# Two pairs of normed token tiles transposed by VectorE blocks and DMA through DRAM instead of TensorE, in a one-core transformer layer

## The chip, the cores and the metric

The kernel runs on one core of one Trainium2 chip. The metric is the device time of one execution, in microseconds (us). The notes below use the names that the profile uses: PE is TensorE (PEld its weight loads), DVE is VectorE, ACT is ScalarE, POOL is GpSimd, and SP is the engine that issues the DMAs of this kernel. "L118" is line 118 of the kernel before.

## The reference: what is computed

1024 tokens of width 512 (float32) pass through three sublayers, each behind a layer norm without weights:

```python
x = L0_attn_hidden_states                       # (4, 256, 512)
x = x + 0.5 * ffn(layernorm(x), A, B, Wr)       # 64 experts of rank 16, 16 of them taken per token
x = x + attn(layernorm(x), wq, wkv, wo)         # 32 heads of 128, causal
x = x + 0.5 * ffn(layernorm(x), A, B, Wr)

def ffn(x):     # per token
    scores = x @ Wr.T;  gates = softmax(top 16 scores);  G = gates placed at their experts
    h = x @ A (64 experts x 16);  out = (h * G) @ B;  return out * 2.0
```

The change lies between the first two sublayers: the normed tokens that the attention reads must be there with the width on the partitions, that is, transposed.

## The kernel before, in words

**Tiles.** The tokens are 8 tiles of 128, taken as 4 pairs. Everything is float32. The large products are made by Strassen-like schemes of seven products (M1 to M7) on sums of blocks, so each operand has to be cut into blocks and added up first.

**First feed-forward layer.** `ffn` (L274 on) runs the pairs through a software pipeline, `for u in range(n + 1)`. In one turn, PE does: the first product `ph_f` of pair u (L354, 7 products of two 128x512 matmuls), the transposes of the gated hidden values of pair u-1 (`pth_f`, L402, 4 groups of four), and its second product `po_f` (L422, 7 products of four 128x256 matmuls, in the order M1, M2, M6, M5, M7, M3, M4). In between lie the norm and router of pair u+1 (`ptx_f` L118, `pr_f` L338, the top-16 gates on DVE L285 to L308, their `exp` on ACT L301, gates L309) and, behind pair u-2, `norm_pair` (L528 on), which prepares the attention's operands. `po_f` M1 reads the block `a11` of `hgT`, M2 the block `a12`. Each block of `hgT` is copied from PSUM by ACT (L403), in the order a11, a21, a22, a12. The sums `hs_f` on DVE (L407 to L411) give M6, M5 and M3 their operands. ACT changes its function table twice in each turn, before the square root of the norms (L97) and before `exp` (L301).

**`norm_pair`.** Its first part makes the statistics (DVE L94, ACT L97 to L104) and writes the normed tokens of both tiles to slots 4 and 5 of `xop[5]` and `xop[6]` (ACT L111). Its second part has PE transpose each tile in four 128x128 matmuls against the identity (`ptx_a`, L118, into a PSUM tile of the pool `ps_t`, which has 2 buffers that `ptx_f` and three of the four `pth_f` groups use as well), and ACT copies the result into the operand blocks: pair 0 with two 128x256 copies per tile (L554, L555), pair 1 with four 128x128 copies per tile (L551, L552), after which DVE makes 8 block sums (`inner_sums`, L171 and the lines before it, called at L560). Pairs 2 and 3 do the same with DVE subtractions that read PSUM (L541 to L548).

**What sets the order.** In this layer a scheduler orders the instructions of each engine when the kernel is built; it may move them across the calls of the code. Each engine then takes its own in that order, and waits at the first that isn't ready. From the attention on, the order is written out by hand (`manual_schedule`) with due times. All DMAs of the kernel are issued by SP in one order. The last of the first layer is the store of the experts' sums (L253); behind it come the first attention weights `wqk` (L608), whose block sums POOL makes (L611).

**A transpose by blocks that is there already.** Late in the attention's `probs`, DVE transposes a 128x384 tile in 32x32 blocks (L1223), SP stores the four bands of 32 partitions to a DRAM tile (`moved`, L1226), and one load brings it back in full order (`pT`, L1232).

Of the kernel before, what the change touches and what calls it, by code (L numbers as in the profile page):

```python
# [9 lines left out]
F32 = mybir.dt.float32  # L10
# [4 lines left out]
P = 128  # L15
# [18 lines left out]
def macaron_kernel(  # L34
# [11 lines left out]
    nc = tc.nc  # L46
# [3 lines left out]
    scratch = ctx.enter_context(  # L50
        tc.tile_pool(name="scratch", bufs=1, space=bass.MemoryType.DRAM)
    )
# [11 lines left out]
    x = const.tile([P, NT, D], F32, tag="x", name="x")  # L64
# [42 lines left out]
    def normed(pool, ts, name, made=None):  # L107

        made = made or [pool.tile([P, D], F32, tag="xn", name=f"xn_{name}_{t}") for t in ts]
        for t, xn, (rstd, bias) in zip(ts, made, norm_stats(ts, f"{name}_{ts[0]}")):  # L110
            nc.scalar.activation(xn, x[:, t, :], AF.Identity, bias=bias, scale=rstd)  # L111
        return made

    def turned_x(xn, name):

        pt = ps_t.tile([P, DC, P], F32, tag="pt", name=f"ptx_{name}")
        for c in range(DC):
            nc.tensor.transpose(pt[:, c, :], xn[:, c * P : (c + 1) * P], ident)  # L118
        return pt

# [151 lines left out]
    def ffn(name, pairs, a_sums, b_sums, after, late, aside=None):  # L274


        with ExitStack() as scope:
# [34 lines left out]
            def prepare(pair):  # L312
# [4 lines left out]
                yield  # L317
                xt = work.tile([P, 2, DC, P], F32, tag="fxT", name=f"fxT_{n}")
                pt = [turned_x(tokens[i], f"{name}_{t}") for i, t in enumerate(pair)]
                for i in range(2):  # L320
                    nc.scalar.copy(xt[:, i], pt[i])
# [182 lines left out]
    xop = [xpool.tile([P, 7, S], F32, tag=f"x{o}", name=f"xop_{o}") for o in range(7)]  # L504


    early = [xop[o][:, 6] for o in (6, 5)]

    def inner_sums(o, eng, between=None):
        blocks = [xop[o][:, i] for i in range(4)]  # L510
        if o < 2:
            blocks[2] = early[o]
        left_sums(
            eng,
            [xop[o][:, i] for i in (4, 5, 6, 2)],
            *blocks,
            pinned=o > 1,
            between=between,
        )
# [8 lines left out]
    def norm_pair(work, pair):  # L528

        half, a = divmod(pair[0] // 2, 2)  # L530
        sl = slice(2 * a, 2 * a + 2)

        where = [xop[k][:, 4:6, :].rearrange("p a s -> p (a s)") for k in (5, 6)]
        tokens = normed(work, pair, "a", where)
        yield
        for i, xn in enumerate(tokens):
            cols = slice(i * P, (i + 1) * P)
            pt = turned_x(xn, f"a_{pair[i]}").rearrange("p (o c) k -> p o c k", o=2)
            a11, a12, s3, a22, s1, _, s2 = (xop[k][:, sl, cols] for k in range(7))
            if half:  # L540
                nc.scalar.copy(a22, pt[:, 1])  # L541
                if a:
                    nc.vector.tensor_tensor(s3[:, 0], early[0][:, cols], pt[:, 0, 0], ALU.subtract)
                    nc.vector.tensor_tensor(s3[:, 1], a11[:, 1], pt[:, 0, 1], ALU.subtract)
                else:
                    nc.vector.tensor_tensor(s3, a11, pt[:, 0], ALU.subtract)
                nc.vector.tensor_tensor(s2, pt[:, 1], s3, ALU.subtract)
                nc.vector.tensor_tensor(s1, a22, pt[:, 0], ALU.add)  # L548
            elif a:
                for o in range(2):  # L550
                    nc.scalar.copy(early[o][:, cols], pt[:, o, 0])  # L551
                    nc.scalar.copy(xop[o][:, 3, cols], pt[:, o, 1])  # L552
            else:
                nc.scalar.copy(a11, pt[:, 0])  # L554
                nc.scalar.copy(a12, pt[:, 1])  # L555
        if half and not a:
            nc.vector.tensor_tensor(xop[5][:, sl], xop[1][:, sl], xop[6][:, sl], ALU.subtract)
        elif a and not half:
            for o in range(2):
                inner_sums(o, nc.vector)  # L560
# [102 lines left out]
    with ExitStack() as scope:  # L663
        experts = load_experts(
            scope, "f1", "right", nc.vector, lambda i: load_x(range(4, NT) if i else (2, 3))
        )
        begin_v(0)
        load_all(("v", 0))
        first_layer = ffn(
            "f1",  # L670
            [(t, t + 1) for t in range(0, NT, 2)],
            *experts[:2],
            after=norm_pair,
            late=True,
            aside=lambda: sum_all(("v", 0), True),
        )
        take(first_layer, 3)
        experts[2]()
# [784 lines left out]
    for p in range(NG):  # L1463
# [34 lines left out]
        else:  # L1498
            steps = merged(p)
            share = sum(cost for _, cost in steps) / 8  # L1500
            parts, t = [[] for _ in range(8)], 0.0
# [130 lines left out]
```

## Time and profile before

| what | us |
|---|---|
| median of three runs (1125.55 to 1126.27) | 1126.14 |
| the profiled execution, its own time | 1124.15 |
| its span in the trace | 1122.3 |
| `ptx_a`: 4 transposes of pair 0, tile 0, start | 68.6 |
| `ptx_a` of pair 1, start | 92.5 |
| first `po_f` products of pairs 1 and 2, start | 72.9 and 100.6 |
| first product of the attention (`pv_a`), start | 127.7 |

The profile is one execution. A row of the groups gives line, engine, operation, tiles with their shapes, count, busy time and mean length. A row of the timeline or of the chain gives its start and length in us from the span's start. Matmuls are pipelined: a row of four transposes is 0.60 us long with its tail, and the next starts 0.44 us after it. The clock granted to TensorE is full speed in all 40 slices of the span. DMA is idle in the slices from 35 to 95 us. For the stretches around the change, the busy time of each engine is:

```profile
58.00:66.00 8.00, 8.00 (x30) 3.98 (x29) 2.78 (x8) 7.67 (x18) 1.06 (x1) 1.00 0.00 0
66.00:74.00 8.00, 8.00 (x49) 5.71 (x48) 4.97 (x28) 5.52 (x15) 2.42 (x3) 1.00 0.00 0
86.00:94.00 8.00, 7.87 (x29) 4.02 (x28) 2.40 (x8) 6.10 (x17) 1.06 (x1) 1.00 0.00 0
94.00:100.00 6.00, 6.00 (x24) 3.32 (x25) 6.00 (x14) 2.51 (x7) 1.06 (x1) 1.00 0.01 2
```

The columns of these rows: stretch and its length, then busy us and instructions of PE, PEld, DVE, ACT and POOL, the granted clock, the DMA engines' share, GB/s.

### The profile page before, as it was taken

The numbers are of one execution on the slowest core, as the hardware profiler recorded it, in microseconds if no ns is written. First come the engines' busy times: TensorE is split into PE (matmuls) and PEld (weight loads), VectorE is DVE, ScalarE is ACT, GpSimd is POOL, SyncE is SP. The second block draws the span as 40 slices with busy tenths as digits, with TensorE's granted clock in tenths as the row PEclk, the third lists the DMA queues.
The fourth block names the chain that finished last, engine by engine and source line by source line (L and its number), as shares of the span: only waits on it lengthen the run. The fifth ranks groups of instructions, "written<-read, shape, count | busy, mean of one in ns | idle before, by whom it ended". The sixth has DMA issues, their size and how long they took to land.

```text
span 1122.3 us, 21075 instructions
## 1 busy us (share of the span) xinstructions
PE 1110.7 (99%) x6834; PEld 977.4 (87%) x6834; DVE 807.3 (72%) x2234; ACT 441.9 (39%) x1328; POOL 626.5 (56%) x870
## 2 busy tenths in 40 slices
PE   9999999999999999999999999999999999999998
PEld 6666888899999999999999998999899999995767
DVE  5554677778778778778778778868778977865432
ACT  4453424444544544544544544544452000107310
POOL 4814487737887887887888788878532000002110
PEclk9999999999999999999999999999999999999999
DMA  9201020156756746746756756655799998750001
GB/s 332 86 1 38 29 67 16 31 145 197 203 138 195 210 136 193 207 136 192 203 152 174 210 144 183 190 166 161 205 311 321 335 348 264 243 180 1 19 19 38
DMA packets 198013, 180.06 MB, mean 160 GB/s; under 512 B 73488, under 2 KB 161296, under 8 KB 197648
## 3 DMA queue, kind: packets, MB, share of 16 engines
q1 hardware_dynamic: 197904, 178.72, 52.5%
q8 instruction: 55, 0.90, 0.3%
q14 instruction: 54, 0.44, 0.1%
HBM read 112.98 MB, written 65.67 MB: 159 GB/s over the span
## 4 chain that ended last, share of the span: by engine, by line
PE 90%; DMA 3%; DVE 2%; POOL 2%; SPq 1%; ACT 1%; issue 1%; POOLq 0%; DVEq 0%
PE po_M L1154 15%; PE po_f L422 9%; PE pqk_c L730 8%; PE ph_f L354 8%; PE pqk_b L730 8%; PE pqk_d L730 7%; PE pa L1255 5%; PE pv_c L829 4%; PE ps L1179 4%; PE pqk_a L730 3%; PE pv_b L829 3%; PE pa L1262 2%; PE ps L1178 2%; PE pv_d L829 2%; PE pv_e L829 2%; PE pv_a L829 2%
## 5 line engine op out<-in xcount | busy, mean ns | idle before, releaser
L384 POOL TENSOR_TENSOR hg_f<-hg_f,gate_f 128x512 f32<-128x512 f32 x32 | 33.5, 1059 | 259.5 <-ACT gate_f L309 151.1
L1154 PE MATMUL po_M<-or_M,ol_M 128*128 128x128 f32 x1456 | 164.7, 275 | 0.0
L1154 PEld LDWEIGHTS po_M<-or_M,ol_M 128*128 128x128 f32 x1456 | 163.7, 192 | 0.1
L611 POOL TENSOR_TENSOR wqk_M<-wqk_M 128x128 f32<-128x128 f32 x320 | 141.7, 458 | 12.1
L747 DVE TENSOR_TENSOR qk<-qk,pqk_d 128x512 f32<-128x512 f32 x210 | 116.6, 561 | 18.9 <-PE pqk_d L730 13.1
L611 POOL TENSOR_TENSOR wqk_M<-wqk_M,wqk_M 128x512 f32<-128x512 f32 (+1 forms) x64 | 107.2, 1683 | 38.7 <-DMA wqk_M<-in_wkv 23.0
L1199 ACT ACTIVATE s<-s,least 128x128 f32<-128x128 f32 (+1 forms) x256 | 114.3, 450 | 21.1 <-DVE least L1187 20.9
L1217 ACT ACTIVATE pn<-s,arden 128x128 f32<-128x128 f32 x220 | 93.7, 426 | 54.4 <-DVE arden L1208 50.7
L730 PE MATMUL pqk_c<-xop,wqk_M 128*128 128x256 f32 x448 | 111.3, 380 | 0.1
L730 PE MATMUL pqk_d<-xop,wqk_M 128*128 128x256 f32 x420 | 106.8, 381 | 1.1 <-DVE qk L747 1.1
L730 PE MATMUL pqk_b<-xop,wqk_M 128*128 128x256 f32 x420 | 104.0, 380 | 0.0
L747 DVE TENSOR_TENSOR qk<-qk,pqk_c 128x256 f32<-128x256 f32 (+1 forms) x112 | 59.7, 533 | 52.2 <-PE pqk_c L730 50.9
L1269 ACT COPY attn<-pa 128x256 f32<-128x256 f32 x128 | 47.4, 371 | 124.4 <-PE pa L1262 121.7
L1054 DVE TENSOR_TENSOR ol_M<-ol_M 128x512 f32<-128x512 f32 x104 | 75.1, 722 | 23.0 <-DMA ol_M<-left 22.6
L747 DVE TENSOR_TENSOR qk<-qk,pqk_b 128x512 f32<-128x512 f32 x105 | 71.7, 683 | 26.7 <-PE pqk_b L730 25.1
L730 PEld LDWEIGHTS pqk_c<-xop,wqk_M 128*128 128x128 f32 x448 | 78.7, 191 | 8.4 <-ACT qk L779 1.2
L1187 DVE CUSTOM_DVE_ANT_0 s<-ps,mask 128x128 f32<-128x128 f32 (+1 forms) x256 | 80.8, 353 | 3.8 <-PE ps L1179 2.6
L730 PEld LDWEIGHTS pqk_d<-xop,wqk_M 128*128 128x128 f32 x420 | 74.1, 191 | 9.9 <-DVE qk L747 2.9
L1255 PE MATMUL pa<-pT,vbuf 128*128 128x256 f32 x256 | 77.5, 384 | 3.4 <-DMA pT<-moved 2.5
L730 PEld LDWEIGHTS pqk_b<-xop,wqk_M 128*128 128x128 f32 x420 | 74.4, 191 | 7.2
L781 POOL TENSOR_TENSOR qk<-qk 128x256 f32<-128x256 f32 x64 | 46.6, 731 | 54.6 <-DVE qk L747 54.0
L1179 PE MATMUL ps<-qk 128*128 128x256 f32 x256 | 76.5, 380 | 0.0
(186 smaller groups left out, 2389.7 us busy)
## 6 DMA issues: line engine op xcount, KB each, us to landing
ol_M<-left SPq DMA_DIRECT2D x52, 512.0 KB, 5.8
moved<-s SPq DMA_DIRECT2D x440, 48.0 KB, 1.7
pT<-moved SPq DMA_DIRECT2D x110, 192.0 KB, 2.7
wv_M<-in_wkv SPq DMA_DIRECT2D x64, 128.0 KB, 2.6
wqk_M<-in_wq SPq DMA_DIRECT2D x64, 128.0 KB, 2.3
wqk_M<-in_wkv SPq DMA_DIRECT2D x64, 128.0 KB, 2.5
wo<-in_wo SPq DMA_DIRECT2D x16, 512.0 KB, 4.6
left<-attn SPq DMA_DIRECT2D x16, 512.0 KB, 3.3
```

The lines of the kernel that those rows point to most:

```text
L354: nc.tensor.matmul(ps, lhsT=left[m][:, c, :], rhs=a_right[m][:, c, :], start=first and c == 0, stop=c == 1, skip_group_check=True,)
L422: nc.tensor.matmul(ps[:, 0:256], lhsT=left[m][:, c, :], rhs=b_right[m][:, c, :], start=first and c == 0, stop=c == 3, skip_group_check=True,)
L611: return nc.gpsimd.tensor_tensor(to, a, b, ALU.subtract)
L730: nc.tensor.matmul(ps[:, i * S : (i + 1) * S], lhsT=right[m][n], rhs=xop[OUTER[m]][:, INNER[n]], start=first and i == 0, stop=True, skip_g ...
L747: nc.vector.tensor_tensor(to, of, ps, ALU.add)
L829: nc.tensor.matmul(ps[:, i * S + t * P : i * S + (t + 1) * P], lhsT=xop[OUTER[m]][:, INNER[n], t * P : (t + 1) * P], rhs=right[m][n], star ...
L1154: nc.tensor.matmul(banks[at // 2][:, cols : cols + P], lhsT=lhsT, rhs=rhs, start=k % 4 == 0 and g == 0 and at % 2 == 0 and t == 0, stop=Tr ...
L1179: nc.tensor.matmul(ps[:, P : 3 * P], lhsT=qT[:, P : 2 * P], rhs=kT, start=True, stop=True)
L1187: nc.vector.tensor_tensor_reduce(out=s[:, cols], in0=ps[:, cols], in1=mask_f[:, cols], scale=-SCALE, scalar=-TAKEN, op0=ALU.add, op1=ALU.m ...
L1199: nc.scalar.activation(s[:, cols], s[:, cols], AF.Exp, bias=least[:, i : i + 1], scale=-1.0, accum_out=den[:, i : i + 1],)
L1217: nc.scalar.mul(pn[:, :, i : 2 * i + 1, :].rearrange("p k t c -> p t k c"), s[:, cols].rearrange("p (t k c) -> p t k c", k=4, c=32), rden[ ...
L1255: nc.tensor.matmul(po[:, 0 : 2 * P], lhsT=v_of(p, j, 2 * b), rhs=of[:, 0:2], start=True, stop=False,)
```

## The change

For pairs 0 and 1 (`half` is 0), the first part of `norm_pair` now also moves each tile: DVE transposes the 128x512 tile in 32x32 blocks from `xop[5]` or `xop[6]` to slots 4 and 5 of `xop[2]` or `xop[3]`; SP stores its four bands of 32 partitions to a DRAM tile `moved_x` (64 KB each), and one load of 256 KB brings it back to where the normed tokens were. The PE transposes `ptx_a` of these two pairs are gone, and with them four uses of the PSUM pool `ps_t`. ACT makes the same number of copies with the same sizes, from SBUF instead of PSUM. Pairs 2 and 3 are left as they were.

```diff
+    def move_x(xn, blocks, name):
+        moved = scratch.tile([P, 4, P], F32, tag="moved_x", name=f"moved_x_{name}", bufs=4)
+        nc.vector.transpose(
+            blocks.rearrange("p (q c r) -> p q c r", q=4, r=32),
+            xn.rearrange("p (c q r) -> p q c r", q=4, r=32),
+        )
+        for t in range(4):
+            nc.sync.dma_start(
+                moved[:, t].rearrange("(q r) x -> r q x", r=32),
+                blocks[32 * t : 32 * t + 32].rearrange("r (q x) -> r q x", q=4),
+            )
+        nc.sync.dma_start(xn, moved.rearrange("p t x -> p (t x)"))
...
         tokens = normed(work, pair, "a", where)
+        if not half:
+            for i, xn in enumerate(tokens):
+                move_x(xn, xop[2 + i][:, 4:6, :].rearrange("p a s -> p (a s)"), f"a_{pair[i]}")
         yield
         for i, xn in enumerate(tokens):
             cols = slice(i * P, (i + 1) * P)
-            pt = turned_x(xn, f"a_{pair[i]}").rearrange("p (o c) k -> p o c k", o=2)
+            if half:
+                pt = turned_x(xn, f"a_{pair[i]}").rearrange("p (o c) k -> p o c k", o=2)
+            else:
+                pt = xn.rearrange("p (t o c x) -> p o c t x", t=4, o=2, x=32)
...
             elif a:
                 for o in range(2):
-                    nc.scalar.copy(early[o][:, cols], pt[:, o, 0])
-                    nc.scalar.copy(xop[o][:, 3, cols], pt[:, o, 1])
+                    for to, k in ((early[o], 0), (xop[o][:, 3], 1)):
+                        nc.scalar.copy(to[:, cols].rearrange("p (t x) -> p t x", t=4), pt[:, o, k])
             else:
-                nc.scalar.copy(a11, pt[:, 0])
-                nc.scalar.copy(a12, pt[:, 1])
+                for to, k in ((a11, 0), (a12, 1)):
+                    nc.scalar.copy(to.rearrange("p c (t x) -> p c t x", t=4), pt[:, k])
```

The scheduler builds a new order from this, on PE, DVE, ACT and SP, between about 59 us and the first product of the attention; ahead of it and behind it, and on POOL throughout, the orders are the same. In the new order:

- **DVE** has the two block transposes of a pair right behind the reciprocal of its norm (L101). For pair 0 this is ahead of the norm statistics of the first layer's last pair (tiles 6 and 7); for pair 1, ahead of the `hs_f` sums of pair 2. The 8 block sums of `inner_sums` come behind the first two `po_f` additions of pair 2 instead of ahead of its `hs_f` sums.
- **ACT**, around pair 0: the copies `hg_f`, `hg_f`, `hgT_f` (a11), then the norm of tiles 6 and 7, two `fxT_f` copies, `hgT_f` (a21), the first operand copy of pair 0, the table load, two `exp`, the second operand copy, `hgT_f` (a22), two gates, the third and fourth operand copies, `hgT_f` (a12), `hg_f`. Before, a21, `hg_f`, a22 and a12 were next to each other behind the gates. Around pair 1: the four `hgT_f` copies, four operand copies, one `hg_f`, four operand copies.
- **PE**, around pair 0: `pth_f` (one group), four `ph_f` matmuls, eight `ptx_f`, one `ph_f`, `pr_f`, `pth_f`, one `ph_f`, two `pth_f` groups, then `po_f`.
- **SP**: the 20 DMAs of `move_x` lie between L253 and the first `wqk` load. Within a pair the order is four stores of the first tile, three of the second, the load of the first, the last store of the second, the load of the second.

## The prediction

> **What bounds the kernel now.** I read the page's busy times first, then the chain that ended last, then that chain in order of time around the change, then ACT, DVE and SP in the timeline of the same stretch.
>
> ```profile
> PE 1110.7 (99%) x6834; PEld 977.4 (87%) x6834; DVE 807.3 (72%) x2234; ACT 441.9 (39%) x1328; POOL 626.5 (56%) x870
> PE 90%; DMA 3%; DVE 2%; POOL 2%; SPq 1%; ACT 1%; issue 1%; POOLq 0%; DVEq 0%
> ```
>
> PE is busy nearly all the time and carries 90% of the chain, so what is taken from PE is gained, unless a wait takes its place. The chain from 41 us on shows one such wait, then the stretch of pair 0 (`ptx_a` at 68.60 and 69.91) and that of pair 1 (92.47):
>
> ```profile
> 42.36 1.28 ACT L301
> 43.65 0.55 ACT pr_f L301 x2
> 44.21 1.00 ACT hgT_f L403 x2
> ...
> 62.75 0.44 PE pth_f L402 x4
> 63.19 0.91 PE ph_f L354 x2
> 64.10 0.61 PE ptx_f L118 x4
> ...
> 68.60 0.44 PE ptx_a L118 x4
> 69.05 0.86 PE ph_f L354 x2
> 69.91 0.44 PE ptx_a L118 x4
> ...
> 73.37 0.48 PE pth_f L402 x4
> 73.85 11.76 PE po_f L422 x54
> 85.61 6.87 PE ph_f L354 x16
> 92.47 0.87 PE ptx_a L118 x8
> ...
> 100.58 12.09 PE po_f L422 x56
> ```
>
> From 62.75 on PE doesn't stop. At 42 to 45 us it does: there the table load and the two `exp` stand ahead of two `hgT_f` copies on ACT, and PE waited 0.84 us for them. SP is free between these two rows of its timeline, which is where the new DMAs go:
>
> ```profile
> 30.29 0.33 SPq L253 DMA_DIRECT2D kept_b<-bt_f  x1
> 98.89 0.37 SPq L608 DMA_DIRECT2D wqk_M<-in_wq  x1
> ```
>
> **What is removed: 16 transposes on PE.** In the chain, 4 take 0.44 us, 8 take 0.87; two pairs make 0.44 + 0.44 + 0.87 = 1.75 us on the path. Here a rule has to be weighed. The Trainium skill, TensorE: Matmul & The Clock Gate, Part 4 (PE-mode transpose), gives about 390 ns for a 128x128 transpose alone and about 275 ns within a kernel. The rows agree with the 275 (`ptx_a` has a mean of 275 ns), but that is the length of one with its tail, and the next starts 110 ns later. By the page's numbers 16 would be worth 4.4 to 6.2 us, by the rows 1.75. I take 1.75. The new order also puts fewer changes of operation on PE. In the stretch of pair 0, rows that are longer than their kind (0.91 for 0.86 twice, 0.61 for 0.44, 0.48 for 0.44) hold 0.31 us of small waits; in that of pair 1 it is 0.13 of "issue" and 0.19 in a `pth_f` row, again 0.3. These may go or return: 0 to 0.62 us.
>
> **What is added on DVE: four block transposes of 128x512.** The nearest row is the one of 128x384 in the attention, which reads PSUM:
>
> ```profile
> L1223 DVE STREAM_TRANSPOSE s<-pn x110: 574/577/580, 220.7 to 804.7; 128x384 f32<-128x384 f32 x110
> ```
>
> Bounds for 512 columns: 0.58 us (no dependence on size) and 0.77 (in proportion); I take 0.71. They wait for ACT's normed tokens, so in pair 0 the first runs from 61.5, the second from 62.2 to 62.9. Queued behind them on DVE are the statistics of tiles 6 and 7, which before ran from 60.1 to 61.8. They now take 62.9 to 64.5; the square root, reciprocal and biases on ACT and DVE end at 65.5, and the normed tiles on ACT at 66.3 and 67.0 (0.8 us each, starts 0.7 apart). PE reaches `ptx_f` in its new order at 62.75 + 0.44 + 4 x 0.86 = 66.63 and 67.07. So this cover holds, with 0.3 and 0.07 us to spare; at 0.77 us each the second would be 0.05 late. In pair 1 they run from 91.25 to 92.65 with the `hs_f` sums behind them, which wait for ACT until 94.5 anyway: nothing.
>
> **What is added on SP and DMA.** In the attention four such stores are issued in 1.76 us, land 1.7 us after issue (median; 1.6 to 4.8), and the load lands after 2.7 (2.3 to 5.4). Those move 48 and 192 KB; 64 and 256 KB in an idle stretch I put at 1.7 and 2.9. Pair 0: seven stores from 62.2 to 65.3, the fourth landed at 65.2, first load 65.3 to 68.2; last store at 65.7, landed 67.4, second load to 70.3. ACT comes to the first copy at 71.0 and to the third at 74.4, so the DMAs are covered by 2.8 and 4.1 us. Pair 1: transposes ended at 91.95 and 92.65, loads landed at 98.1 and 100.5. ACT then makes the eight copies by 101.3. DVE needs them for the block sums at 103.3, behind the addition of M2; the sums (8 x 0.335 us) end at 106.0, and the addition of M6 queued behind them at 106.4, just when PE wants that bank for M7 (106.4). Nothing, but with no cover left: a load 2 us later would stop PE. Behind the DMAs on SP stand the `wqk` loads; SP is free for them at 97.8, before 98.89, so they don't move.
>
> Against this way stands the Trainium skill, VectorE: DVE Perf Modes, Rules for kernel authors: a 128x128 transpose belongs on TensorE where PSUM will do as a target, and VectorE is for 32x32. The rows say why it needn't hold here: DVE has free time (2.8 of 8 us busy from 58 to 66) and PE none.
>
> **What moves: the copies on ACT, and this becomes a wait.** PE in the new order, from 62.75 with the lengths of the rows: `pth_f` 0.44, four `ph_f` 3.44, `ptx_f` 0.88, `ph_f` 0.86, `pr_f` 1.68, `pth_f` 0.44 (ends 70.49), `ph_f` 0.86, `pth_f` 0.88 (72.23), `po_f` M1 1.74: 73.97. M2 then reads a12. ACT: a21 from 70.5, next start 0.5 later; first operand copy 71.0 (0.38); table load 1.28; two `exp` 0.5; second operand copy 0.27; a22 0.5; two gates 0.5; two operand copies 0.54; a12 0.59, done at 75.6. That is a wait of 1.65 us for M2, the same kind as the 0.84 at 42 to 45 us. Before, M2 began at 73.85 + 6 x 0.218 = 75.16. So M2 starts 75.6 instead of 75.16, about 0.45 later, although PE has 0.88 less to do. M6 wants an `hs_f` sum at 77.3 that is done at 75.7: covered. If the table load took the 2.7 us of the Trainium skill, ScalarE: Activation LUTs, Table sets, M2 would start at 77.0; all rows of this trace say 1.28, which I take.
>
> For pair 1 there is no table load in between, and the four `hgT_f` copies come first: a12 is done at 95.7 and needed at 101. PE from 92.47: three `pth_f` groups, `ph_f`, `pth_f`, three `ph_f`, half of M1, two `ph_f`, rest of M1, together 8.65 us, so M2 at 101.1 instead of 100.58 + 1.73 = 102.3, a gain of 1.2 if the small waits vanish, 0.9 if they return.
>
> **Sum.** -1.75 for the transposes, -0.62 to 0 for the small waits, +1.65 for M2: -0.7 to -0.1, I take -0.4. Behind 130 us the orders are the same, and POOL's chain that follows (163 to 183 us) starts from products of PE, so the difference is carried to the end. The profiled execution (1124.15, its span and 1.85 us around it) would go to 1123.75; the median lies 1.99 above, hence 1125.7.
>
> **Rivals.**
> - **The wait doesn't form** (0.12). ACT would have to have a12 by 74. For it: before, ACT was idle 2.45 us at 66 to 69. Against: a12's copy stands behind nine others and a table load. Then -1.75 to -2.4: 1124.0.
> - **A longer wait at M2** (0.20). The 0.07 us of cover of `ptx_f` fails, copies from SBUF with runs of 32 are slower than the 0.37 us from PSUM, small waits return. Four copies of 0.2 more and 0.5 on PE's way to `pth_f` give +1.3: 1127.0.
> - **The round trip comes late, slower than before** (0.10). Place: the first and third operand copy of pair 0 on ACT, with `exp` and the `hgT_f` copies behind them. It decides from the moment a load lands after 71.0 or 74.4. At the longest landings seen in the attention (4.8 and 5.4 us) the first load lands at 73.7 and the second at 78.9, M2 waits 4.5 us more: 1130.2. Against: those landings are under 150 to 220 GB/s, here DMA is idle.
> - **The change doesn't do what it says**: the built order has no `ptx_a` left for these pairs; no chance kept.
>
> **How the numbers follow.** Likeliest, 0.58: 1125.7. About 0.2% (2.25 us) is what a measurement of this kernel can tell from no change. Faster by that needs 1123.9, which only the first rival in full can give: 0.05. Slower needs 1128.4: the late round trip and a tail of the longer wait, 0.13. Within it: 0.82. The range leaves out the late round trip and the last of the full gain: 1124.0 to 1127.9.
>
> **What would show it.** Right: an idle time of PE in front of a `po_f` row at about 74 us, ended by ACT `hgT_f`, of 1.2 to 2 us; ACT's copies of pair 0 not ended by a DMA; block transposes of about 0.7 us; no wait at 106 us. Wrong: ACT's operand copies waiting for `moved_x`, PE waiting at `ptx_f`, or the difference arising behind 130 us.

## The result, and the profile after

| | before | after |
|---|---|---|
| median of five runs each, us | 1125.66 (1124.39 to 1126.27) | 1131.48 (1130.12 to 1132.01) |
| the profiled execution, its own time, us | 1124.15 | 1130.17 |
| its span, us | 1122.3 | 1128.4 |

The ratio is 1.0057, with a 95% interval of 1.0046 to 1.0067: slower by 5 to 7.5 us, where 1125.7 was forecast and 1127.9 was the upper end of the range.

The page of the changed kernel has PE busy for 0.8 us less than before, and less of the chain on PE; DVE, ACT and DMA each have a point more of it.

```profile
PE 1109.9 (98%) x6818; PEld 975.9 (86%) x6818; DVE 813.0 (72%) x2238; ACT 443.0 (39%) x1328; POOL 626.3 (56%) x870
PE 89%; DMA 4%; DVE 3%; ACT 2%; POOL 2%; SPq 1%; issue 1%; POOLq 0%; DVEq 0%; ACTq 0%
```

Its chain in order of time (start, length, what) answers to the rows from 62.75 on that the prediction shows. Lines are shifted: L354 is now L369, L402 L417, L422 L437; L418 is the `hgT_f` copy, L576 an operand copy of pair 0, L186 a block sum, L449 the addition of a `po_f` product to `x`.

```profile
67.62 0.66 PE ptx_f L118 x4
...
71.35 0.59 ACT hgT_f L418
71.94 0.30 ACT xop L576
...
72.26 1.28 ACT L316
...
75.41 0.60 ACT xop L576 x2
76.00 0.49 ACT hgT_f L418
...
76.54 10.63 PE po_f L437 x48
87.16 6.87 PE ph_f L369 x16
...
104.46 0.42 DVE x L449
104.88 4.79 DVE xop L186 x8
109.67 0.34 DVE x L449
...
110.05 1.99 PE po_f L437 x8
```

The chain leaves PE twice. From 71 to 76.5 us it runs over ACT, which is the wait for M2 that was predicted. From 104.5 to 110 it runs over DVE: eight block sums take 4.79 us and hold up the addition that frees the bank of M7. The timeline of PE has both waits with their lengths, in the brackets:

```profile
76.54 1.78 PE L437 MATMUL po_f<-b_f,hgT_f 128*128 128x256 f32 x7 [1.76 <-ACT hgT_f L418]
...
110.05 1.99 PE L437 MATMUL po_f<-bt_f,hgT_f 128*128 128x256 f32 x8 [2.07 <-DVE x L449]
```

Where the 6.1 us of the span come from is read off four marks: the first `pth_f` of the second pair's hidden values, the first `ph_f` of the next turn, the first product of the attention (`pv_a`), and the end.

| stretch | before | after | difference |
|---|---|---|---|
| start to `pth_f` (62.59, 63.13), nothing changed here | 62.59 | 63.13 | +0.5 |
| turn of pair 0, to `ph_f` (85.44, 87.00) | 22.85 | 23.87 | +1.0 |
| turn of pair 1, to `pv_a` (127.53, 130.30) | 42.09 | 43.30 | +1.2 |
| attention to the end | 994.8 | 998.1 | +3.3 |

The first is from one execution to the next: in the 14 traces of this study in which nothing is changed ahead of it, that mark lies from 62.1 to 63.4. So the change itself lost 2.2 us where it was made. In this pair of traces the larger part, 3.3 us, lies behind 130 us, where the orders are the same as before; two traces can't size that part well, as the table of experiments shows.

### The profile page after: what moved, and what is told of

The parts are those of the page before. It is cut to its first block, busy times and chain, and to the rows that moved or that the text cites. A ratio compares the mean times of both kernels' runs of the same rounds, so it can differ in the third digit from the quotient of the medians.

```text
span 1128.4 us, 21070 instructions
## 1 busy us (share of the span) xinstructions
PE 1109.9 (98%) x6818; PEld 975.9 (86%) x6818; DVE 813.0 (72%) x2238; ACT 443.0 (39%) x1328; POOL 626.3 (56%) x870
## 4 chain that ended last, share of the span: by engine, by line
PE 89%; DMA 4%; DVE 3%; ACT 2%; POOL 2%; SPq 1%; issue 1%; POOLq 0%; DVEq 0%; ACTq 0%
PE po_M L1175 15%; PE pqk_b L751 8%; PE pqk_c L751 8%; PE ph_f L369 8%; PE po_f L437 8%; PE pqk_d L751 7%; PE pa L1276 5%; PE pv_c L850 4%; PE ps L1200 4%; PE pqk_a L751 4%; PE pv_b L850 3%; PE pa L1283 2%; PE ps L1199 2%; PE pv_a L850 2%; PE pv_d L850 2%; PE pv_e L850 2%
## 5 line engine op out<-in xcount | busy, mean ns | idle before, releaser
L632 POOL TENSOR_TENSOR wqk_M<-wqk_M 128x128 f32<-128x128 f32 x320 | 142.3, 459 | 12.1
L632 POOL TENSOR_TENSOR wqk_M<-wqk_M,wqk_M 128x512 f32<-128x512 f32 (+1 forms) x64 | 107.4, 1688 | 42.1 <-DMA wqk_M<-in_wkv 25.2
L1200 PE MATMUL ps<-qk 128*128 128x256 f32 x256 | 76.5, 380 | 0.0
```

What stands on the lines that cost most here:

```text
L632: return nc.gpsimd.tensor_tensor(to, a, b, ALU.subtract)
L1200: nc.tensor.matmul(ps[:, P : 3 * P], lhsT=qT[:, P : 2 * P], rhs=kT, start=True, stop=True)
```

## The experiments

In the table, "turns" is the time from `pth_f` to `pv_a` (64.94 before), and "attention" that from the first to the last copy of an attention product (693.4 before). Both are from one trace each; the ratio is against the kernel before, run beside it; it is estimated from all executions and need not be that of the two medians.

| kernel | us, before beside it | ratio, 95% | turns | attention |
|---|---|---|---|---|
| changed kernel | 1131.48, 1125.66 | 1.0057 (1.0046 to 1.0067) | 67.2 | 696.4 |
| pair0_only | 1127.99, 1124.92 | 1.0024 (1.0014 to 1.0034) | 65.9 | 695.4 |
| pair1_only | 1128.53, 1124.92 | 1.0034 (1.0021 to 1.0047) | 67.9 | 696.4 |
| same_addresses | 1131.26, 1124.92 | 1.0052 (1.0036 to 1.0067) | 68.9 | 695.3 |
| gap_1MiB | 1124.94, 1124.92 | 1.0001 (0.9993 to 1.0009) | 64.9 | 693.7 |
| pool_waits | 1126.54, 1124.50 | 1.0020 (1.0014 to 1.0027) | 65.1 | 694.7 |
| copies_and_sums_late | 1127.22, 1124.50 | 1.0027 (1.0016 to 1.0038) | 65.7 | 694.9 |
| dmas_only | 1125.61, 1124.50 | 1.0011 (1.0002 to 1.0019) | 64.9 | 695.0 |
| delay_only | 1126.83, 1124.50 | 1.0018 (1.0011 to 1.0024) | 67.9 | 693.3 |
| order_by_hand | 1127.46, 1125.47 | 1.0020 (1.0012 to 1.0029) | 63.3 | 697.0 |
| dmas_twice | 1125.29, 1125.47 | 1.0002 (0.9992 to 1.0012) | 64.9 | 696.8 |
| dmas_small | 1124.47, 1125.47 | 1.0000 (0.9990 to 1.0010) | 64.9 | 694.8 |
| dmas_early | 1125.82, 1125.47 | 1.0002 (0.9992 to 1.0012) | 64.9 | 694.5 |
| order_by_hand_padded | 1126.44, 1125.04 | 1.0011 (1.0003 to 1.0019) | 63.3 | 697.0 |
| dve_six_more | 1125.93, 1125.04 | 1.0010 (1.0001 to 1.0018) | 64.9 | 695.5 |
| pe_fourteen_less | 1130.40, 1125.04 | 1.0044 (1.0030 to 1.0057) | 64.9 | 695.7 |
| pe_64_more | 1131.24, 1125.04 | 1.0052 (1.0038 to 1.0066) | 64.9 | 695.5 |

The last two kernels start later by 3.4 and 5.9 us at the first mark, which the two last columns don't contain. The turns of pair1_only and same_addresses contain 1.7 us of a lower clock, told below. The last column has to be read with care: the ten traces without the change (the kernel before included) lie from 693.3 to 696.8, the eight with it from 694.7 to 697.0, so that no single trace separates them. The ratios do: less what the turns, the start and the lower clock explain, they leave 1.7 to 3.9 us behind `pv_a` with the change, and -0.9 to 1.6 without it.

### One pair at a time

```diff
-        if not half:
+        if not half and not a:
             for i, xn in enumerate(tokens):
...
-            if half:
+            if not (not half and not a):
                 pt = turned_x(xn, f"a_{pair[i]}").rearrange("p (o c) k -> p o c k", o=2)
```

This is pair0_only; pair1_only has `a` for `not a`. The other pair is transposed on PE again.

> Only pair 0 is moved by VectorE and DMA; pair 1 is transposed by TensorE as before. The traces show two local losses: M2 of the second product of pair 1 starts about 1.0 us later against the start of that turn (its operand copy stands behind the table load and the operand copies on ScalarE), and TensorE waits 2.07 us for a VectorE addition behind the block sums of pair 1. Theory 1 (the losses are local and each belongs to its pair): this kernel keeps the first alone: the wait of 1.76 us ended by ScalarE hgT_f is there, the wait of 2.07 us is not, and at the first product of the attention it is about 1.0 us later than before. Theory 2 (the two pairs interact, for instance the first delay makes the second collision): neither this nor the kernel with pair 1 alone shows the wait of 2.07 us. For the whole time: 1.0 us over before if all is local, 3 to 4 us if what the attention adds (about 3 us in the first trace) comes with any such DMA or with the moved DRAM tiles.

> Only pair 1 is moved by VectorE and DMA. Theory 1 (local losses): TensorE gains about 1.2 us up to the second product of pair 2 and then waits about 2 us there for the VectorE addition behind the block sums, which take about 0.8 us each in their middle, since GpSimd's weight sums run at that time, instead of 0.35; at the first product of the attention it is 0.9 us later than before, and ScalarE shows no new wait at the first product's turn of pair 0. Theory 2 (interaction): no wait there, so 1.2 us earlier than before. For the whole time: 0.9 us over before if all is local, 3 to 4 us if the attention adds its part here too.

Measured: 1.0024 and 1.0034; the two losses, 2.7 and 3.8 us, add up to the 6.4 of both (0.0057 of 1125). pair0_only has the wait at M2 (1.76 us) and none at M7, with 1.0 us more in the turns; pair1_only has the wait of 2.07 us at M7 and none at M2. So each wait belongs to its pair. In both the attention of the trace is 2 to 3 us longer.

### The DRAM tile: where the attention's tiles lie

The new tile `moved_x` shifts the attention's DRAM tiles by 1 MiB. One kernel has the new order with the old addresses (`moved_x` lies in rows of the output that are written later), the other the old order with the shift.

```diff
-        moved = scratch.tile([P, 4, P], F32, tag="moved_x", name=f"moved_x_{name}", bufs=4)
+        at = int(name.split("_")[1]) * P
+        moved = out[at : at + P].rearrange("p (t x) -> p t x", t=4)
```

```diff
         take(first_layer, 3)
         experts[2]()
+        gap = scratch.tile([P, 4, 4, P], F32, tag="gap", name="gap")
+        nc.sync.dma_start(gap[:, 0, 0, 0:64], wr_sb[:, 0, :])
```

> The changed kernel, with its orders of instructions on all engines, but the blocks pass through the rows of the output tensor (written with the result at the end) instead of tiles of their own in DRAM. So every later DRAM tile of the attention has the address that it has in the kernel before; in the changed kernel these are 1 MiB higher. Theory A (what the attention adds, about 3 us, comes from the addresses): about 2.2 us over before, with the two local waits, and an attention as long as before. Theory B (it comes with the later phase or with the 20 DMAs, not with the addresses): about 5.8 us over before, like the changed kernel.

> The kernel before, with its orders of instructions, plus a DRAM tile of 1 MiB that nothing reads (one store of 32 KB goes to it at a time when no DMA runs), so that the later DRAM tiles of the attention have the addresses of the changed kernel. Theory A (addresses): about 3 us over before, all of it in the attention, with TensorE waiting longer for the loads of pT. Theory B: like before, within 0.5 us.

Measured: 1.0052 with the old addresses, like the changed kernel; 1.0001 with the shift alone (at most 0.0009, or 1.0 us). The addresses are not the cause.

The trace of same_addresses showed something else. Its timeline of PE around M7, with the wait in brackets:

```profile
109.98 2.88 PE L438 MATMUL po_f<-bt_f,hgT_f 128*128 128x256 f32 x8 [2.07 <-DVE x L450]
112.65 2.73 PE L438 MATMUL po_f<-b_f,hs_f 128*128 128x256 f32 x8
115.22 1.89 PE L438 MATMUL po_f<-bt_f,hgT_f 128*128 128x256 f32 x8
```

Eight such matmuls take 1.89 us with their tail, 1.99 right behind a wait. The first two rows take 2.88 and 2.73: 1.7 us are lost once more, since the clock that was granted fell to half. The busy times of the engines around it, with the columns as for the kernel before (the granted clock is the third number from the end):

```profile
107.50:110.90 3.40, 1.33 (x7) 0.91 (x6) 2.76 (x6) 0.00 (x0) 3.08 (x7) 1.00 0.00 0
110.95:114.35 3.40, 3.40 (x9) 2.66 (x8) 0.42 (x1) 0.00 (x0) 3.32 (x8) 0.50 0.00 0
114.40:117.80 3.40, 3.40 (x21) 3.04 (x20) 1.07 (x3) 0.32 (x1) 3.40 (x6) 1.00 0.02 5
```

The trace of pair1_only has the same from 109.35 to 112.76, 3.68 us for the row behind the wait. The clock does not fall every time: 2 of the 5 executions of the changed kernel, 4 of 6 of same_addresses and 1 of 6 of pair1_only have a mean clock of 0.998, none of the 21 of pool_waits below. In same_addresses those four take 1130.7 to 1133.3 us, the other two 1128.2 and 1128.3. The profiled execution of the changed kernel is one without it.

The traces show what decides. In them the clock changes only in steps of 3.413 us: its stretches, the last of a trace aside, are whole numbers of these, such as 102.40, 105.81, 1116.16 and 3.413 us (30, 31, 327 and 1). Counted in such steps from the first rise of the clock (at 5.12 us in same_addresses, 6.95 in pair1_only and 6.67 in the changed kernel), the pause of 2.07 us lies within one step in the first two, and the next step ran at half the clock. In the changed kernel it is divided between two steps, 1.09 and 0.98 us, and the clock stayed. The pause of 1.76 us at M2 lies within one step in three traces (pair0_only, same_addresses, pool_waits), and the clock stayed there too. If the place of the pause is left to chance, it lies within one step in (3.41 - 2.07) / 3.41 = 39% of the executions (an estimate); seen were 7 of 17, if the pause is behind all of these. A mean of 0.998 also stands in one execution each of pair0_only, of order_by_hand_padded and of the kernel before (of 158), which have no such pause; where their clock fell is not known.

### Who slows the block sums

The theory after the first runs: GpSimd. Its sums of the first attention weights (`wqk_M`, L632) run at the same time as DVE's block sums, which they did not before. The rival: the sums are slow because they come right after the copies and the DMAs of pair 1. In one kernel GpSimd waits for the last block sum (a small copy reads it, and `True` keeps the first weight sum behind that copy); in the other the sums and the copies of pair 0 come later in the code, with GpSimd left alone.

```diff
     load_all(("qk", 0))
+    seen = const.tile([P, 1], F32, tag="seen", name="seen")
+    tc.keep_in_program_order(nc.gpsimd.tensor_copy(seen, xop[1][:, 2, 0:1]))
-    sum_all(("qk", 0))
+    sum_all(("qk", 0), True)
```

```diff
                     take(steps, 8)
+                    take(behind, 1)
...
         yield
+        if not half and not a:
+            yield
         for i, xn in enumerate(tokens):
...
         elif a and not half:
+            yield
+            yield
             for o in range(2):
```

> The changed kernel with one small copy more on GpSimd (128x1), which reads the last of the block sums of pair 1 and stands ahead of GpSimd's first weight sums of the attention, so that GpSimd is idle while VectorE makes the block sums. All other orders are the same. Theory A (the middle block sums take 0.8 us instead of 0.35 because GpSimd adds from the same memory at that time): all eight take 0.34 to 0.42 us each, the addition of M6 comes 2 us earlier, and TensorE's wait of 2.07 us ahead of M7 shrinks to under 0.3 us; whole time about 2 us less than the changed kernel, 3 to 4 us over before. Theory B (they are slow for another reason, such as what the DMA brought or which operands they read): they stay at 0.8 us and the wait stays.

> The changed kernel with two of its steps placed later: the second to fourth operand copies of pair 0 stand behind all hgT_f copies on ScalarE, and the addition of M6 stands between the block sums of pair 1 on VectorE instead of behind them. Theory A (local waits of the two turns): the wait ahead of M2 falls from 1.8 us to about 1.2 (the table load and one operand copy still stand ahead), that of 2.07 us goes; TensorE is at the attention's first product within 0.5 us of before, and the whole time is 2.5 to 3 us less than the changed kernel. If the attention's part (2 to 3 us more than before in all kernels with the moves so far) is a thing of its own, 2 to 3 us over before stay. Rival (the attention's part follows from the lateness at its start): nothing over before stays.

First the kernel before: the block sums on DVE, while GpSimd has nothing between 91 and 98 us, and then the first weight sums on GpSimd:

```profile
93.98 1.09 DVE L171 TENSOR_TENSOR xop<-xop,xop 128x256 f32<-128x256 f32 x3 [4.06 <-ACT xop L551]
94.99 1.42 DVE L171 TENSOR_TENSOR xop<-xop 128x256 f32<-128x256 f32 x4
96.33 0.41 DVE L171 TENSOR_TENSOR xop<-xop,xop 128x256 f32<-128x256 f32 x1
...
103.51 1.28 POOL L611 TENSOR_TENSOR wqk_M<-wqk_M,wqk_M 128x512 f32<-128x512 f32 x1
104.86 3.84 POOL L611 TENSOR_TENSOR wqk_M<-wqk_M 128x128 f32<-128x128 f32 x8
```

In the changed kernel, DVE:

```profile
104.79 1.09 DVE L186 TENSOR_TENSOR xop<-xop,xop 128x256 f32<-128x256 f32 x3
105.80 3.27 DVE L186 TENSOR_TENSOR xop<-xop 128x256 f32<-128x256 f32 x4
109.00 0.67 DVE L186 TENSOR_TENSOR xop<-xop,xop 128x256 f32<-128x256 f32 x1
109.59 0.74 DVE L449 TENSOR_TENSOR x<-x,po_f 128x256 f32<-128x256 f32 x2
```

and GpSimd:

```profile
105.54 1.47 POOL L632 TENSOR_TENSOR wqk_M<-wqk_M,wqk_M 128x512 f32<-128x512 f32 x1 [1.41 <-DMA wqk_M<-in_wkv]
107.09 4.37 POOL L632 TENSOR_TENSOR wqk_M<-wqk_M 128x128 f32<-128x128 f32 x8
```

The row of four sums hides two kinds. The first two of them, and the GpSimd sum between, looked at alone:

```profile
105.80 1.49 DVE L186 TENSOR_TENSOR xop<-xop 128x256 f32<-128x256 f32 x1
107.21 0.67 DVE L186 TENSOR_TENSOR xop<-xop 128x256 f32<-128x256 f32 x1
107.09 0.52 POOL L632 TENSOR_TENSOR wqk_M<-wqk_M 128x128 f32<-128x128 f32 x1
```

Both inputs of a block sum lie in `xop`. The first three sums take 1.09 us as before. From 105.54 on, when GpSimd begins, four take 3.27 instead of 1.42. GpSimd is slowed too: 1.47 and 4.37 us for what takes 1.27 and 3.83 alone. But DVE's two additions at 109.59, one of whose inputs is in PSUM, take 0.74 us together, no longer than usual (0.42 for one, the next 0.33 behind it), although GpSimd is still busy. In pool_waits, DVE and then GpSimd:

```profile
104.28 1.09 DVE L186 TENSOR_TENSOR xop<-xop,xop 128x256 f32<-128x256 f32 x3
105.28 1.43 DVE L186 TENSOR_TENSOR xop<-xop 128x256 f32<-128x256 f32 x4
```

```profile
107.11 0.18 POOL L1296 COPY seen<-xop 128x1 f32<-128x1 f32 x1 [3.50 <-DVE xop L186]
107.31 1.27 POOL L632 TENSOR_TENSOR wqk_M<-wqk_M,wqk_M 128x512 f32<-128x512 f32 x1
108.66 3.83 POOL L632 TENSOR_TENSOR wqk_M<-wqk_M 128x128 f32<-128x128 f32 x8
```

With GpSimd held back, all eight sums are at their old speed at the same place, behind the same copies and DMAs; PE reaches M7 at 107.43 without a wait, and the kernel is at 1.0020. In copies_and_sums_late GpSimd begins 0.37 us behind the first sum, so the first three already take 2.16 us, and 0.66 us of wait stay at M7. The theory holds, the rival falls. The Trainium skill, SBUF — State Buffer, section SBUF: two separate sides, has the rule for this: DVE and GpSimd share a pair of SBUF ports, and a DVE operation with two SBUF inputs and a GpSimd operation that reads SBUF shut each other out for the whole instruction. The rows agree in kind: the sum of 105.80 ends 0.28 us behind GpSimd's large operation (107.01), so it waited for all of that, and the addition with an input in PSUM is not touched. Behind that the two engines take turns, one sum of each in 0.60 us (DVE's start at 107.21, 107.81, 108.40 and 109.00). That is less than the two take alone one after the other, 0.34 on DVE and 0.48 on GpSimd (3.83 / 8), so beside the small sums they do not shut each other out for quite the whole instruction.

copies_and_sums_late also has pair 0's copies behind the `hgT_f` copies, and its wait at M2 is 0.93 instead of 1.76 us. What is left of it is the table load ahead of the a12 copy. In exchange PE waits 0.52 us for an `hgT_f` copy of the next pair at 117 us.

### Why the attention is longer

In pool_waits the turns are at 65.1 us, as long as in the kernel before (64.9), but the kernel is 2.2 us slower. Candidates: the 20 DMAs that come earlier on SP's queue (in dmas_only at 55 to 62 and 85 to 91 us, some 8 us earlier than in the changed kernel), and the later start of the attention that most of these kernels have. dmas_only is the kernel before with these DMAs, which nobody reads; delay_only is the kernel before with 13 idle matmuls ahead of the attention.

```diff
         tokens = normed(work, pair, "a", where)
+        if not half:
+            for i, t in enumerate(pair):
+                moved = scratch.tile([P, 4, P], F32, tag="moved_x", name=f"moved_x_{t}", bufs=4)
+                for k in range(4):
+                    nc.sync.dma_start(
+                        moved[:, k].rearrange("(q r) x -> r q x", r=32),
+                        x[32 * k : 32 * k + 32, t, :].rearrange("r (q x) -> r q x", q=4),
+                    )
+                nc.sync.dma_start(
+                    xop[2 + i][:, 4:6, :].rearrange("p a s -> p (a s)"), moved.rearrange("p t x -> p (t x)")
+                )
```

```diff
+    held = ps_s.tile([P, 512], F32, tag="s", name="held")
+    for _ in range(13):
+        nc.tensor.matmul(held[:, 0:P], lhsT=zeros, rhs=zeros, start=True, stop=True)
     first_products(2)
```

> The kernel before with the 20 DMAs added and nothing else: the tokens of pairs 0 and 1 (not normed) go to DRAM in the same bands and come back in slots that nobody reads. The orders on TensorE, VectorE, ScalarE and GpSimd are those of before. Theory A (the attention is longer because these DMAs ran earlier on the same queue[...]): first layer as before, attention 2 to 3 us longer with longer waits for the loads of pT, whole time 2 to 3 us over before. Theory B (the attention is longer because it begins later or with a different spacing of the engines): like before within 0.5 us.

> The kernel before with 13 idle 128x128 products on TensorE ahead of the attention's first product, about 2.8 us, and nothing else of note (four instructions change places with a neighbour on ScalarE, VectorE and GpSimd right behind that point). Theory A (the attention's part comes from the DMAs): 2.8 us over before and an attention as long as before. Theory B (a later start alone makes the attention longer): 5 to 6 us over before.

Measured: delay_only costs 2.0 us, not more than the 2.9 by which its attention starts later, so a later start is not the cause. dmas_only costs 1.2 us (0.2 to 2.1), with the turns unchanged. That looked like half of it. Three variants of it followed: all 20 DMAs twice, 20 of 2 KB each, and the same 20 in a row, meant for about 31 us.

```diff
                 for k in range(4):
-                    nc.sync.dma_start(
-                        moved[:, k].rearrange("(q r) x -> r q x", r=32),
-                        x[32 * k : 32 * k + 32, t, :].rearrange("r (q x) -> r q x", q=4),
-                    )
+                    nc.sync.dma_start(moved[0:4, k], x[0:4, t, 0:P])
```

That is dmas_small, whose loads are cut in the same way. dmas_twice has the block of dmas_only two times, and dmas_early has it, for tiles 0 to 3, behind `experts[2]()`.

> The kernel before with the transfers of the change issued twice, 40 of them with 64 and 256 KB, unread. If the number or the bytes of earlier transfers lengthen the attention, it is about twice as much as with 20: +2 to +3 us, attention 696. If what counts is the position that the transfers of the attention then take[...], it may be anything from 0 to 2 us. If the +1.1 us of the 20 was chance, 0.

> The kernel before with 20 transfers at the same places that move 2 KB each instead of 64 and 256 KB, unread. If the bytes or the descriptors of the 20 transfers lengthen the attention: 0. If it is their number: +1.1 us, attention 695.

> The kernel before with the same 20 transfers of 64 and 256 KB, unread, but issued in a row at about 31 us, behind the stores of the experts' sums, instead of around pairs 0 and 1. If it is what they leave behind on the queue that lengthens the attention: +1.1 us again, attention 695. If it is their nearness to the attention or to the first attention weights: 0.

Measured: 1.0002, 1.0000, 1.0002. dmas_early did not do what it was made for: in its trace the DMAs run at 55 to 62 and 85 to 91 us, not at 31, so it is dmas_only over again, and the cost isn't there this time. Twice the DMAs show no cost either (the interval ends at 1.0012, or 1.4 us), so the +1.2 of dmas_only can't be put down to them. The trace of dmas_twice warns of something else: its attention has 696.8 us, 3.4 more than before, in an execution of 1127.0 at a median of 1125.29. One trace is one draw.

In one more kernel all that was known was put together: GpSimd waits, pair 0's copies come later, and in the third turn the a12 block is copied second, ahead of the table load.

```diff
-                for i, j in ((0, 0), (1, 0), (1, 1), (0, 1)):
+                second = pair == pairs[1]
+                for i, j in ((0, 0), (0, 1), (1, 0), (1, 1)) if second else ((0, 0), (1, 0), (1, 1), (0, 1)):
...
+                        if second:
+                            nc.vector.tensor_tensor(s4, a12, s2, ALU.subtract)
-                    elif (i, j) == (0, 1):
+                    elif (i, j) == (0, 1) and not second:
```

> The changed kernel with three repairs of its order: GpSimd waits for the block sums; pair 0's operand copies come behind the hgT copies on ACT; and the third turn copies the a12 block second, ahead of the table load, so that M2 finds it (s4 is then made from the copied a12). If the two stalls of PE are what the change costs, the waits at M2 and M7 are gone, pv_a starts 1.5 to 2.5 us earlier than in the kernel before after allowing for the start-up, and the gain of 1.75 us that was predicted appears there. What stays is the longer attention (1 to 2 us by the runs so far), so 1123.5 to 1125 against 1124.5 to 1125: the same within 0.2%. If the attention is only longer because a stall or a delay precedes it, its length falls back to 693.5 and the kernel is 1.5 to 2.5 us faster than before.

Its timeline of PE around M1 and M2, and around M7:

```profile
71.56 1.04 PE L418 MATMUL pth_f<-ident,hg_f 128*128 128x128 f32 x8
72.43 3.62 PE L440 MATMUL po_f<-b_f,hgT_f 128*128 128x256 f32 x16
75.97 1.13 PE L440 MATMUL po_f<-b_f,hs_f 128*128 128x256 f32 x4
...
105.52 0.27 PE L418 MATMUL pth_f<-ident,hg_f 128*128 128x128 f32 x1
105.75 1.99 PE L440 MATMUL po_f<-bt_f,hgT_f 128*128 128x256 f32 x8
```

No bracket in these rows: both waits are gone, and `pv_a` comes 63.32 us behind `pth_f` instead of 64.94. So without the waits the turns are 1.62 us shorter, near the 1.75 that the prediction had for the transposes. And yet the kernel takes 2.2 us more than the one before (1.4 to 3.3): some 3.9 us are lost in the attention. The longest waits of PE there are of one kind in all kernels; for the kernel before, the changed one and order_by_hand, in that order:

```profile
PE pa L1255 <- DMA pT<-moved: 2.5, 6, 0.6
```

```profile
PE pa L1276 <- DMA pT<-moved: 4.8, 8, 1.0
```

```profile
PE pa L1282 <- DMA pT<-moved: 4.4, 9, 1.0
```

(us in all, times, longest.) PE waits for the round trips of `probs` through DRAM, the four stores of `moved` and the load of `pT`. A load is issued when its stores have landed. Added up over the 110 of them, the time from the end of DVE's transpose to the issue of the load is 514 us before, 525 in the changed kernel and 529 in order_by_hand. Over 18 traces, this sum and the length of the attention go together with a correlation of 0.90. So the longer attention comes with longer round trips, and with longer waits of PE for them; what sets them off was not found. In all traces PE keeps within 0.4 us of the kernel before up to 250 us. The kernel before is the quickest of the 18 traces to 400 us, and most of the loss of the changed kernel and of order_by_hand comes between 300 and 400 us and again between 750 and 800.

One more candidate: with other numbers of instructions ahead of the attention (as built, PE 22 fewer, DVE 6 more), the engines may fetch their instructions at other moments, and these fetches are DMA too (the page of before lists 109 packets of kind instruction, 1.3 MB). Four runs shift the streams without the change, or take the shift of PE out of order_by_hand.

```diff
     for _ in range(14):
         nc.tensor.matmul(idle[:, 0:P], lhsT=zeros, rhs=zeros, start=True, stop=True)
+    for _ in range(19):
+        nc.tensor.matmul(idle[0:1, 0:1], lhsT=zeros[:, 0:1], rhs=zeros[:, 0:1], start=True, stop=True)
```

That is order_by_hand_padded; pe_64_more has 64 of them in the kernel before. pe_fourteen_less is the kernel before without the loop of 14; dve_six_more has six fills of one column of `zeros` behind its memset.

> The repaired version (order_by_hand) with 19 matmuls of a single number put at its head, among the idle ones, so that PE's instruction stream has as many instructions as in the kernel before (3988). If the attention is longer because PE's instruction blocks are fetched at other moments, it falls back to about 693.5 to 694.5 us and the kernel gains 2 us or more against order_by_hand: 1124 or less, faster than before by 1 us or so. If PE's position in its stream is not the cause: 1.002 again.

> The kernel before with 6 tiny fills on DVE at the head, so that DVE's stream has as many instructions as in the changed kernel. If the moments at which DVE's instruction blocks are fetched lengthen the attention: +1 to +3 us. If not: 0.

> The kernel before without the 14 idle matmuls at the head, so that PE's stream is shifted by 14 of the 22 instructions that the change and its scheduling take away. If PE's fetch moments lengthen the attention: +1 to +3 us there. If not: 0, apart from what the idle matmuls themselves are worth at the start (seen ahead of the attention).

> The kernel before with 64 matmuls of a single number at the head, a shift of PE's stream the other way. If fetch moments matter, the attention may change by 1 to 3 us either way; if not, 0, apart from a later start.

Measured: the padded version is at 1.0011 (0.3 to 2.1 us above the kernel before), but its trace has the same attention as without padding, 697.0 us, and it is not the gain that was expected. dve_six_more costs 1.1 us (0.1 to 2.0), in the attention if anywhere. pe_fourteen_less starts 3.4 us later and costs 5.0, pe_64_more starts 5.9 later and costs 5.9; its late start is not the number of instructions alone, since the granted clock was at half from 8.8 to 19.0 us. So shifts of the streams are worth between 0 and 1.6 us, and none comes to the 2 to 4 us. The candidate is not supported as the one cause; a share of 1 to 2 us can't be excluded. That several small parts (the DMAs, the shifts on PE and on DVE) add up was not tested.

No version with the change beats the kernel before; the best, order_by_hand_padded, is above it by 0.11%, with an interval that leaves out equality.

## Why the prediction was wrong

The forecast for the two turns was a gain of 0.4 us; they lost 2.2. Behind them the forecast was nothing, and by the ratio some 3 us went there.

**What is removed** was right: 1.75 us for 16 transposes by the spacing of the rows, where the length of one in the Trainium skill (TensorE: Matmul & The Clock Gate, Part 4) would have given 4.4 to 6.2. Without the two waits, the turns are shorter by 1.62.

**The block transposes** take 0.71 us each, as put. The cover of 0.07 us for the second `ptx_f` of pair 0 did not hold: the row has 0.66 us instead of 0.44. PE waiting there was one of the prediction's own signs of being wrong.

**The DMAs** of pair 0 were covered, as put: no copy of pair 0 on ACT was ended by one. They came later than put in pair 1, where the loads are issued at 96.98 and 100.08, and ACT waits for both (2.55 and 0.72 us). The term that was too small is the last store of a pair: issued behind the first load, it took 2.9 us to land for pair 0 and 2.6 for pair 1, where 1.7 was put. SP's timeline of the changed kernel:

```profile
93.52 3.23 SPq L130 DMA_DIRECT2D moved_x_a<-xop  x7
96.98 0.34 SPq L134 DMA_DIRECT2D xop<-moved_x_a  x1
97.37 0.42 SPq L130 DMA_DIRECT2D moved_x_a<-xop  x1
100.08 0.34 SPq L134 DMA_DIRECT2D xop<-moved_x_a  x1
100.47 0.43 SPq L629 DMA_DIRECT2D wqk_M<-in_wq  x1
```

The whole turn began 1.5 us later than in the prediction (87.16 for 85.61). ACT's last copy of pair 1 ended at 103.64, and the block sums begin at 104.79 behind the addition of M2, so the loads were still in time for DVE; pool_waits shows it too, with no wait at M7. The `wqk` loads did move, from 98.89 to 100.47, and with them GpSimd's first weight sum, from 103.51 to 105.54.

**The wait for M2** was right in kind, place and size: 1.76 us, ended by ACT `hgT_f`, at 74.8 to 76.5, for 1.65 predicted. The turn lost 1.0 us instead of 0.45, with the 0.11 here, the 0.22 at `ptx_f` and 0.2 where PE starts anew.

**The step that failed first** is the term for pair 1's block sums: "the sums (8 x 0.335 us) end at 106.0, and the addition of M6 queued behind them at 106.4 ... Nothing, but with no cover left". The order and the place were right: allowing for the 1.5 us by which the turn was late, sums from 103.3 and an addition that is wanted at 106.4 become 104.8 and 107.9, and the trace has 104.79 and PE waiting from 107.98. The duration was wrong. 0.335 us is the row of the kernel before, where GpSimd stood idle. Moved by 10 us, the sums fell into GpSimd's weight sums, which the trace of before shows from 103.51 on, and took 4.79 us instead of 2.68. With no cover, all 2.1 us of that became PE's wait of 2.07: instead of the 0.9 to 1.2 us that this turn was to gain, it lost 1.2. In some executions the lower clock behind the wait took 1.7 more. The prediction had named this place as the one without cover, but for a late load; it asked which instructions stand on DVE's queue, but not what runs on the engine beside it at the new time.

**The step that failed second**: "Behind 130 us the orders are the same ... so the difference is carried to the end". The orders are the same; the time is not. By the ratios, the kernels with the change lose 1.7 to 3.9 us behind `pv_a`, those without it -0.9 to 1.6. Longer round trips through DRAM go with it. The addresses, the number and size of the earlier DMAs and the later start each showed no cost of that size (the intervals of gap_1MiB, dmas_twice and delay_only leave up to 1.0, 1.4 and 0 us); the shifts of the instruction streams reached 1.6 at most. What the cause is stays open.

**The rivals**: the longer wait at M2 (1127.0) had the cover of `ptx_f` right, for 0.2 us, but not the slower copies from SBUF (0.39 to 0.41 us for 0.37). The late round trip (1130.2) comes nearest in time, but not for its reason: no copy of pair 0 waited for a load.

## What to carry to other kernels

A duration from a profile holds for the neighbours that the instruction had there. When a change moves a DVE operation with two inputs in SBUF to another time, look at what GpSimd does at that time, and where no cover is left, don't count the operation at its old length: here a sum of 0.34 us became one of 0.60 beside GpSimd's small sums, and waited out a whole large one. And when work is removed from an engine that is busy for 99%, only a kernel with the new waits taken out (here 1.62 us of 1.75) shows whether the sum was right; where the rest of the program waits for DMAs at a few places, 2 to 4 us of 1125 can still go there for reasons that its order of instructions doesn't show.

## What was new about the hardware

- DVE and GpSimd stop each other on operations with SBUF inputs alone: a DVE sum every 0.60 us for 0.34 beside GpSimd's sums of 128x128, one of 1.49 us beside a sum of 128x512, and 4.37 for 3.83 on GpSimd; not with an input in PSUM.
- A pause of PE of 2.07 us can be enough for half the clock behind it, for 3.41 us, at a cost of 1.7 us: in both traces where the pause lay within one of the clock's steps of 3.413 us, and not in the one where it was divided between two. Pauses of 1.76 us within one step left the clock alone in three traces. The Trainium skill, TensorE: Matmul & The Clock Gate, Part 1 (What's actually happening), puts the idle window at some 3.4 us; the steps here are as long, but PE need not be idle for all of one.
- The 14 idle matmuls at the head are worth 3.4 us at the first mark. Without them (pe_fourteen_less) the first rows of PE are 1.5 to 1.8 times as long:

```profile
7.14 1.94 PE L116 MATMUL ptx_f<-ident,xn_f 128*128 128x128 f32 x8 [7.14 <-ACT xn_f L109]
8.90 3.68 PE L336 MATMUL pr_f<-wr_sb,fxT_f 128*128 128x64 f32 x16
```

  With them, the same two rows take 1.27 and 2.00 us.
